# Attention stage on one Trainium2 core: the keys' mean taken from ScalarE's accumulator, eight heads' maxima placed together, and values weighed in halves in the steps without a piece

## The chip, the cores and the metric

The program runs on one core of a Trainium2 chip. The time is the device time of one execution in microseconds (us). Before the change three runs gave 1661.81, 1661.89 and 1663.59 us, so the median is 1661.89 us. One further execution was profiled; it took 1659.83 us, of which the span from the first to the last instruction is 1658.1 us. Lines of the code are named as the profile names them: L367 is line 367 of the kernel before.

## What is computed

A block of four parts runs on an input of 8 batches x 512 tokens x 256 channels: an attention that only treats the more telling queries, a routed feed-forward layer, a gated linear attention with its own feed-forward layer, and the routed layer again. The change lies in the attention alone:

```python
q, k, v = (_split_heads(x @ W + b) ...)            # 16 heads of 16 channels
scores = jnp.einsum('bhqd,bhkd->bhqk', q, k) * scale
sparsity = scores.max(axis=-1) - scores.mean(axis=-1)
_, top_idx = jax.lax.top_k(sparsity, U)            # U = 307 of 512 queries
attn = jax.nn.softmax(scores_sel, axis=-1)
out_sel = jnp.einsum('bhuk,bhkd->bhud', attn, v)   # the other queries give zero
```

The kernel does not form the mean of the scores. It takes the mean over the tokens off the keys, so that the maximum of the scores against these keys is at once "maximum minus mean".

## The kernel before

**Layout.** The 16 heads of a batch stand in two key tiles `ks[0]` and `ks[1]` and two query tiles `qs[0]`, `qs[1]` (parity e), each of two halves m of 128 rows. A half holds four blocks of 32 rows, and a block holds one head's 16 rows of that parity and one spare row. The spare row of the keys is one, the spare row of the queries takes the negated maximum, so that the score product of the second pass comes out less its maximum.

**Two passes in lockstep.** The loop at L539 runs over steps n. Step n takes the maxima (`max_one`, L415) of four heads for 128 queries: four score products on TensorE into PSUM banks of the pool `bank_m` (four banks), four maxima on VectorE (L425). The same step takes the exponentials (`exp_one`, L429) of the heads and keys of step n - 16 (`LAG`): four score products on TensorE (L433) into the pool `bank` (three banks), four exponentials on ScalarE (L437). A step sends its products in two halves of four (exp 0, max 1, exp 2, max 3; then max 0, exp 1, max 2, exp 3). The products of a half sit on the four row groups of TensorE and run side by side. Between the halves TensorE weighs the values with the exponentials of the step before (`finish`, `weigh`, L442). A batch is 16 steps; with 8 batches there are 128 steps, and then 16 more with exponentials alone.

**Pieces.** Behind each step one piece of the projections of a later batch is sent (`front`, L271): the generator yields after each piece. For a batch these are two transposes of the normalized input (`xnT`), then for m = 0 the two halves of the query projection, the mean of the keys (`km`), the two halves of the key projection, for m = 1 the same without the mean, and four pieces for the values: 15 pieces in 16 steps. I number the places behind the steps of a batch 0 to 15 (n - 14 modulo 16): before, place 4 is the mean, place 15 is empty. A projection piece is held in a bank of `bank_m` until its copy is written.

**The keys' mean before.** The copy of the transposed input on ScalarE (L298) also sums the tokens; four small products on TensorE (L344) carry the sum through the key weights; four small VectorE operations (L350 to L355) make the bias `kb`; ScalarE writes the two key tiles with it (L367).

**Placing the maxima.** When the four steps of one (m, e) are done, `place_maxima` (L396) runs two steps later: TensorE turns the 16 columns of maxima, ScalarE negates them (L403), SP issues four transfers into the spare query rows and four into `neg`, the table for the choice of the queries. It runs in the steps of places 3, 7, 11 and 15.

**Start and end.** The first 14 steps (`LEAD`) have maxima only, while the pieces of batches 0 and 1 are sent faster. In the last steps, 113 to 128, the batches to project are used up, and in three of four steps `finish` runs in two halves of 256 queries, one behind each half of the scores (`halves`, L543). After the last maximum VectorE finds the queries to drop in 26 rounds (`top_queries`, L464), while TensorE and ScalarE do the last 16 steps of exponentials; the rest of the program follows.

**Order.** Each engine runs its instructions in the order in which this code sends them. There is no reordering; what the code puts behind a waiting instruction of an engine waits too.

Of the kernel before, what the change touches and what calls it, by code (L numbers as in the profile page):

```python
# [17 lines left out]
P = 128  # L18
# [20 lines left out]
def block_kernel(ctx: ExitStack, tc: tile.TileContext, t: dict, out: bass.AP):  # L39
# [59 lines left out]
    with ExitStack() as outer:  # L99
# [20 lines left out]
        neg = a_out.tile([P, L], F32, name="neg")  # L120
        mx = a_out.tile([P, NB, NG, 4 * 4], F32, name="mx")
        work = a_out.tile([P, L + 8], F32, name="work")
        m8 = a_out.tile([P, 8], F32, name="m8")

        with ExitStack() as inner:
# [60 lines left out]
            for e in range(2):  # L186
                nc.vector.tensor_scalar(bq_own[:, e, :], bq, own[:, e : e + 1], None, ALU.mult)


# [81 lines left out]
            def front(b, pick, alone):  # L271
# [18 lines left out]
                xnT = a2.tile([P, NC2, L], F32, tag="xnT", name=f"xnT{b}")  # L290
                xsum = a2.tile([P, NC2], F32, tag="xsum", name=f"xsum{b}")
                for c in range(NC2):
                    ps = pick(f"xnT_ps{b}")
                    for k in range(4):
                        nc.tensor.transpose(
                            ps[:, bass.ts(k, P)], xn[:, k, bass.ts(c, P)], ident
                        )
                    nc.scalar.activation(  # L298
                        xnT[:, c, :], ps, AF.Identity, accum_out=xsum[:, c : c + 1]
                    )  # L300
                    yield
# [10 lines left out]
                fronts[b] = (qs, ks, va)  # L312
                kb = a2.tile([P, 2, NC2], F32, tag="kb", name=f"kb{b}")

# [6 lines left out]
                for m in range(NC2):  # L321
                    ps = pick(f"q_ps{b}")
                    for c in range(NC2):
                        project(ps, wq, m, c)
                        if c == 0:
                            yield
                    for e in range(2):
                        if alone and (b > 0 or e == 0):
                            nc.scalar.activation(
                                qs[e][:, m, :], ps, AF.Identity,  # L330
                                bias=bq_own[:, e, m : m + 1], scale=own[:, e : e + 1],
                            )
                        else:
                            nc.vector.tensor_scalar(
                                qs[e][:, m, :], ps, bq[:, m : m + 1], own[:, e : e + 1],
                                ALU.add, ALU.mult,
                            )
                    yield
                    if m == 0:

                        pm = pick(f"km_ps{b}")
                        for mm in range(NC2):
                            for c in range(NC2):
                                nc.tensor.matmul(  # L344
                                    pm[:, mm : mm + 1], wk[:, c, bass.ts(mm, P)],
                                    xsum[:, c : c + 1],
                                    start=(c == 0), stop=(c == NC2 - 1),
                                )
                        km = a2.tile([P, NC2], F32, tag="km", name=f"km{b}")
                        nc.vector.scalar_tensor_tensor(  # L350
                            km, pm[:, 0:NC2], 1.0 / L, bk, ALU.mult, ALU.add
                        )
                        nc.vector.tensor_tensor(km, bk, km, ALU.subtract)
                        for e in range(2):
                            nc.vector.tensor_scalar(  # L355
                                kb[:, e, :], km, kept[:, e : e + 1], one[:, e : e + 1],
                                ALU.mult, ALU.add,
                            )
                        yield

                    ps = pick(f"k_ps{b}")
                    for c in range(NC2):
                        project(ps, wk, m, c)
                        if c == 0:
                            yield
                    for e in range(2):
                        nc.scalar.activation(  # L367
                            ks[e][:, m, :], ps, AF.Identity,
                            bias=kb[:, e, m : m + 1], scale=kept[:, e : e + 1],
                        )  # L370
                    yield
# [23 lines left out]

            def place_maxima(b, m, e):  # L396


                q = fronts[b][0][e]
                pt = bank_m(f"mxT_ps{b}")  # L400
                nc.tensor.transpose(pt[0:16, 0:P], mx[:, b, 2 * e + m, :], ident)
                negT = a2.tile([16, P], F32, tag="negT", name=f"negT{b}")
                nc.scalar.mul(negT, pt[0:16, 0:P], -1.0)  # L403
                r = b * H + 8 * e + 4 * m
                for k in range(4):
                    nc.sync.dma_start(
                        out=q[DH * (1 - e) :: 32, m, bass.ts(k, P)],
                        in_=negT[4 * k : 4 * k + 4, :],
                    )
                for k in range(4):  # L410
                    nc.sync.dma_start(
                        out=neg[r : r + 4, bass.ts(k, P)], in_=negT[4 * k : 4 * k + 4, :]
                    )

            def max_one(b, m, e, k, j, pick):  # L415
# [9 lines left out]
                nc.vector.tensor_reduce(  # L425
                    mx[:, b, 2 * e + m, r : r + 1], s, AX.X, ALU.max
                )
# [69 lines left out]
            def maximum_of(n):  # L497

                b, m, e, k = steps[n]
                return mx[0:1, b, 2 * e + m, 4 * k : 4 * k + 1]  # L500

# [37 lines left out]
            for n in range(len(steps) + LAG + 1):  # L539
                ahead = steps[n] if n < len(steps) else None  # L540
                here = steps[n - LAG] if 0 <= n - LAG < len(steps) else None
                es = [None] * 4
                halves = 96 <= n - LAG - 1 < 112 and (n - LAG - 1) % 4 > 0  # L543
                if ahead is None:
# [30 lines left out]
                if n < LEAD:  # L575
# [6 lines left out]
                    for _ in near.get(n, ()):  # L582
                        pass
                    while done < 23 * (n + 1) // LEAD:
                        next(pieces, None)
                        done += 1
                else:
                    if n >= LAG:
                        next(later, None)
                    b, i = divmod(n - LEAD, 16)  # L590
                    if i == 0:
                        for _ in pieces:
                            pass
                        pieces = front(b + 2, bank_m, False) if b + 2 < NB else iter(())
                    next(pieces, None)

# [676 lines left out]
```

## Time and profile before

| what | value |
|---|---|
| median of three runs | 1661.89 us |
| profiled execution, its span | 1659.83 us, 1658.1 us |
| first maximum starts | 20.71 us |
| steps 0 to 13 (maxima only) | 20.7 to 65.4 us, VectorE busy 42.3 of 44.7 us |
| one batch of 16 steps | 67.4 us |
| last maxima (step 127) | from 536.6 us |
| choice of the queries on VectorE | 546 to 588 us |
| share of the span: TensorE, VectorE, ScalarE, GpSimd | 97%, 58%, 41%, 20% |

PE is TensorE's matrix products and PEld its weight loads, DVE is VectorE, ACT ScalarE, POOL GpSimd, SP the engine that issues most transfers. A line of the timeline gives start, length, engine, source line, operation, and the tile written and the tiles read. A product of 32-bit numbers appears as two instructions (x2 for one projection, x8 for four products of values). Lengths of neighbouring rows overlap, since engines start an instruction before the last one has ended; the distance from start to start is what one costs.

### The profile page before, as it was taken

Reading aid. Unit: us, or ns where it says so; the run is one execution under the profiler, and the core shown is the slowest. Engines: PE = TensorE matmul, PEld = TensorE weight load, DVE = VectorE, ACT = ScalarE, POOL = GpSimd, SP = SyncE. Lnnn points to the kernel's source line nnn. Section 1 sums busy time; section 2 is a strip of 40 time slices with the busy share of each in tenths; the row PEclk is TensorE's granted clock in tenths of the full one; section 3 lists DMA queues with packets and bytes.
Section 4 is the critical chain, followed back from the end, with each engine's and each line's share of the span. In section 5 each row is a group of like instructions: output and inputs, shape, how many; then the busy total and the mean of one; then the engine's idle time right before and its main releaser. Section 6 shows DMA issues by size and latency. Waiting matters only on the chain.

```text
span 1658.1 us, 19533 instructions
## 1 busy us (share of the span) xinstructions
PE 1605.9 (97%) x7298; PEld 823.9 (50%) x7298; DVE 968.2 (58%) x2007; ACT 680.1 (41%) x1216; POOL 334.8 (20%) x384
## 2 busy tenths in 40 slices
PE   7999999999999969999989999999999999999999
PEld 3423323333233247655564556555655655766666
DVE  6977777676666785437663566267265533344242
ACT  2366666666656814352346123622521452121110
POOL 3011111010100112114342342144233320000000
PEclk9999999999999979999999999999999999999999
DMA  3100000000000051010000001000000010011100
GB/s 108 40 2 3 3 2 3 2 3 2 2 3 3 2 164 26 6 34 13 1 1 0 1 1 27 0 0 0 1 1 1 0 26 0 20 33 37 41 26 26
DMA packets 23234, 27.55 MB, mean 17 GB/s; under 512 B 4932, under 2 KB 19684, under 8 KB 23140
## 3 DMA queue, kind: packets, MB, share of 16 engines
q1 hardware_dynamic: 22068, 24.74, 5.1%
q10 hardware_dynamic: 1072, 1.57, 0.3%
q8 instruction: 57, 0.93, 0.2%
q14 instruction: 37, 0.30, 0.1%
HBM read 21.19 MB, written 4.33 MB: 15 GB/s over the span
## 4 chain that ended last, share of the span: by engine, by line
PE 77%; DVE 14%; ACT 3%; POOL 3%; issue 2%; DMA 1%; SPq 0%; ACTq 0%; POOLq 0%; DVEq 0%
PE y_ps L891 16%; PE h_ps L911 11%; PE s L433 8%; PE s L422 8%; PE swi_ps L938 7%; PE proj_ps L1021 7%; PE av L442 7%; DVE pr L1054 2%; DVE pr L1044 2%; PE ao_ps L780 2%; DVE mx L425 2%; PE gla_y L1146 2%; PE q_ps L316 2%; PE v_ps L376 2%; PE k_ps L316 2%
## 5 line engine op out<-in xcount | busy, mean ns | idle before, releaser
L425 DVE TENSOR_REDUCE mx<-s 128x1 f32<-128x512 f32 x512 | 329.0, 684 | 129.0 <-PE s L433 83.0
L437 ACT ACTIVATE e<-s 128x512 f32<-128x512 f32 x512 | 276.1, 599 | 179.1 <-PE s L433 103.5
L422 PE MATMUL s<-k,q 32*128 32x512 f32 x1024 | 298.9, 638 | 2.5 <-ACT k L367 1.8
L433 PE MATMUL s<-q,k 32*128 32x512 f32 x1024 | 294.3, 638 | 0.4 <-DVE mx L425 0.3
L891 PE MATMUL y_ps<-w,h 128*128 128x256 f32 x1024 | 232.2, 382 | 3.5 <-DVE h L920 3.5
L911 PE MATMUL h_ps<-xnT,w 128*128 128x512 f32 x512 | 230.3, 598 | 4.1 <-ACT h L919 4.1
L891 PEld LDWEIGHTS y_ps<-w,h 128*128 128x128 f32 x1024 | 194.1, 192 | 40.9 <-issue 11.1
L911 PEld LDWEIGHTS h_ps<-xnT,w 128*128 128x128 f32 x512 | 95.5, 191 | 114.8 <-issue 106.1
L920 DVE TENSOR_TENSOR h<-h,mk 128x512 f32<-128x512 f32 x128 | 97.8, 777 | 82.2 <-ACT h L919 58.3
L442 PE MATMUL av<-e,va 128*32 128x512 f32 (+1 forms) x1120 | 141.9, 568 | 3.8 <-ACT e L437 2.4
L919 ACT ACTIVATE h<-h_ps,b 128x512 f32<-128x512 f32 x96 | 65.5, 684 | 176.9 <-PE h_ps L911 176.8
L422 PEld LDWEIGHTS s<-k,q 32*128 32x128 f32 x1024 | 89.6, 183 | 84.9 <-DVE mx L425 56.5
L896 DVE TENSOR_TENSOR xres<-xres,y_ps 128x512 f32<-128x512 f32 x48 | 32.8, 684 | 163.6 <-PE y_ps L891 149.3
L433 PEld LDWEIGHTS s<-q,k 32*128 32x128 f32 x1024 | 88.1, 183 | 80.8 <-ACT e L437 53.8
L938 PE MATMUL swi_ps<-zT,w_gate 128*128 128x512 f32 x256 | 122.0, 596 | 4.7 <-DVE h L947 4.6
L938 PE MATMUL swi_ps<-zT,w_up 128*128 128x512 f32 x256 | 121.2, 594 | 0.0
L891 PE MATMUL y_ps<-w_down,h 128*128 128x256 f32 x512 | 116.6, 380 | 0.0
L1021 PE MATMUL proj_ps<-q_w,rT 128*128 128x512 f32 x256 | 116.5, 594 | 0.0
L891 PEld LDWEIGHTS y_ps<-w_down,h 128*128 128x128 f32 x512 | 95.8, 190 | 21.1 <-issue 9.5
L944 ACT ACTIVATE h<-swi_ps 128x512 f32<-128x512 f32 x64 | 38.2, 596 | 157.4 <-PE swi_ps L938 157.3
L1071 POOL TENSOR_TENSOR o<-o,pr 128x512 f32<-128x512 f32 (+2 forms) x56 | 81.1, 1449 | 58.9 <-DVE pr L1054 56.9
L802 POOL TENSOR_TENSOR xres<-xres,b 128x512 f32<-128x512 f32 x32 | 40.0, 1268 | 245.5 <-ACT row L742 223.1
(193 smaller groups left out, 1734.6 us busy)
## 6 DMA issues: line engine op xcount, KB each, us to landing
mk<-md SPq DMA_DIRECT2D x32, 256.0 KB
xres<-in_L_attn_a_x SPq DMA_DIRECT2D x8, 512.0 KB
out<-xres SPq DMA_DIRECT2D x16, 256.0 KB
q<-negT SPq DMA_DIRECT2D x128, 2.0 KB
neg<-negT SPq DMA_DIRECT2D x128, 2.0 KB
w<-in_f_w1T SPq DMA_DIRECT2D x1, 1024.0 KB
w<-in_f_w2T SPq DMA_DIRECT2D x1, 1024.0 KB
w_gate<-in_b_w_gateT SPq DMA_DIRECT2D x1, 1024.0 KB
```

The lines of the kernel that those rows point to most:

```text
L316: nc.tensor.matmul(ps, w[:, c, bass.ts(m, P)], xnT[:, c, :], start=(c == 0), stop=(c == NC2 - 1),)
L422: nc.tensor.matmul(s, qs[e][rows, m, bass.ts(k, P)], ks[e][rows, m, :], start=True, stop=True)
L425: nc.vector.tensor_reduce(mx[:, b, 2 * e + m, r : r + 1], s, AX.X, ALU.max)
L433: nc.tensor.matmul(s, ks[e][rows, m, bass.ts(kt, P)], qs[e][rows, m, :], start=True, stop=True)
L437: nc.scalar.activation(ex, s, AF.Exp, scale=1.0 / DH**0.5)
L442: nc.tensor.matmul(av[32 * j : 32 * j + 32, queries], va[:, 8 * kt + 4 * m + j, e, :], es[j][:, queries], start=(kt == 0), stop=(kt == 3 a ...
L891: nc.tensor.matmul(y[0][:, bass.ts(i, D)], h[f][:, bass.ts(2 * u + i, P)], w[:, f, :], start=(f == 0), stop=(f == NF - 1),)
L911: nc.tensor.matmul(ps, w1[:, c, bass.ts(f, P)], xT[g][:, c, :], start=(c == 0), stop=(c == NC2 - 1),)
L920: nc.vector.tensor_tensor(hf, hf, mk[g][:, f, :], ALU.mult)
L938: nc.tensor.matmul(ps, w[:, c, bass.ts(f, P)], zT[g][:, c, :], start=(c == 0), stop=(c == NC2 - 1),)
L1021: nc.tensor.matmul(ps, rT[b // G4][:, c, bass.ts(b % G4, P)], q_w[:, c, m], start=(c == 0), stop=(c == NC2 - 1),)
L1071: nc.gpsimd.tensor_tensor(dst, dst, src, ALU.add)
```

## The change

It does three things.

1. The mean of the keys. `xnT` is copied without a sum, and the `km` piece with its products and VectorE operations is gone. Instead ScalarE first writes a key half with its bias into `ks[0]` and sums it on the way (`accum_out`), makes from the sum two biases of one column each, and then writes the two key halves as before (over the first writing). Two constants, `bk_kept` and `kept_l`, are made once at the start.
2. `place_maxima` takes both parities of a half at once: one transpose of 32 columns, one negation, then eight transfers into the queries and eight into `neg`. Only the last batch's m = 1 goes one by one. `mx` is laid out anew for it.
3. A batch has 14 pieces now. Places 6 and 14 of a batch, and all places once the batches are used up, are empty, and a step with an empty place weighs the values in halves unless it is the first of a group of four.

```diff
-                    nc.scalar.activation(
-                        xnT[:, c, :], ps, AF.Identity, accum_out=xsum[:, c : c + 1]
-                    )
+                    nc.scalar.copy(xnT[:, c, :], ps)
...
-                    if m == 0:
-                        pm = pick(f"km_ps{b}")
...
-                        yield
                     ps = pick(f"k_ps{b}")
                     for c in range(NC2):
                         project(ps, wk, m, c)
                         if c == 0:
                             yield
+                    total = a2.tile([P, 3], F32, tag="total", name=f"total{b}")
+                    nc.scalar.activation(
+                        ks[0][:, m, :], ps, AF.Identity,
+                        bias=bk[:, m : m + 1], accum_out=total[:, 2:3],
+                    )
+                    for e in range(2):
+                        nc.scalar.activation(
+                            total[:, e : e + 1], total[:, 2:3], AF.Identity,
+                            bias=bk_kept[:, e, m : m + 1], scale=kept_l[:, e : e + 1],
+                        )
                     for e in range(2):
                         nc.scalar.activation(
                             ks[e][:, m, :], ps, AF.Identity,
-                            bias=kb[:, e, m : m + 1], scale=kept[:, e : e + 1],
+                            bias=total[:, e : e + 1], scale=kept[:, e : e + 1],
                         )
                     yield
...
-            def place_maxima(b, m, e):
+            def place_maxima(b, m, es):
...
-                nc.tensor.transpose(pt[0:16, 0:P], mx[:, b, 2 * e + m, :], ident)
-                negT = a2.tile([16, P], F32, tag="negT", name=f"negT{b}")
-                nc.scalar.mul(negT, pt[0:16, 0:P], -1.0)
+                n = 16 * len(es)
+                pt = bank_m(f"mxT_ps{b}")[0:n, 0:P]
+                nc.tensor.transpose(
+                    pt, mx[:, b, m].rearrange("p e n -> p (e n)")[:, 16 * es[0] : 16 * es[0] + n],
+                    ident,
+                )
+                negT = a2.tile([32, P], F32, tag="negT", name=f"negT{b}")
+                nc.scalar.mul(negT[0:n, :], pt, -1.0)
...
+            EMPTY = (6, 14)
...
-            for _ in range(7):
+            for _ in range(6):
                 next(first)
...
-                halves = 96 <= n - LAG - 1 < 112 and (n - LAG - 1) % 4 > 0
+                batch, i = divmod(n - LEAD, 16)
+                empty = n >= LEAD and (batch + 2 >= NB or i in EMPTY)
+                halves = empty and LAG < n <= len(steps) and (n - LAG - 1) % 4 > 0
...
                 if ahead is not None and ahead[3] == 3:
-                    full.append((n + 2, ahead[0:3]))
+                    b, m, e = ahead[0:3]
+                    if b == NB - 1 and m == 1:
+                        full.append((n + 2, (b, m, (e,))))
+                    elif e == 1:
+                        full.append((n + 2, (b, m, (0, 1))))
...
-                    while done < 23 * (n + 1) // LEAD:
+                    while done < 22 * (n + 1) // LEAD:
...
-                    next(pieces, None)
+                    if not empty:
+                        next(pieces, None)
```

More of the change, by code (lines that the diff above doesn't have):

```diff
@@ L120, in block_kernel @@
         neg = a_out.tile([P, L], F32, name="neg")
-        mx = a_out.tile([P, NB, NG, 4 * 4], F32, name="mx")
+        mx = a_out.tile([P, NB, NC2, 2, 4 * 4], F32, name="mx")
         work = a_out.tile([P, L + 8], F32, name="work")
@@ L187, in block_kernel @@
                 nc.vector.tensor_scalar(bq_own[:, e, :], bq, own[:, e : e + 1], None, ALU.mult)
+            bk_kept = a1.tile([P, 2, NC2], F32, name="bk_kept")
+            kept_l = a1.tile([P, 2], F32, name="kept_l")
+            for e in range(2):
+                nc.vector.tensor_scalar(
+                    bk_kept[:, e, :], bk, kept[:, e : e + 1], one[:, e : e + 1],
+                    ALU.mult, ALU.add,
+                )
+            nc.vector.tensor_scalar(kept_l, kept, -1.0 / L, None, ALU.mult)
             vas = [
@@ L290, in front @@
                 xnT = a2.tile([P, NC2, L], F32, tag="xnT", name=f"xnT{b}")
-                xsum = a2.tile([P, NC2], F32, tag="xsum", name=f"xsum{b}")
                 for c in range(NC2):
@@ L312, in front @@
                 fronts[b] = (qs, ks, va)
-                kb = a2.tile([P, 2, NC2], F32, tag="kb", name=f"kb{b}")
                 def project(ps, w, m, c):
@@ L338, in front @@
                     yield
-                    if m == 0:
-                        pm = pick(f"km_ps{b}")
[L342 to L358, printed above, removed]
-                        yield
                     ps = pick(f"k_ps{b}")
@@ L365, in front @@
                             yield
+                    total = a2.tile([P, 3], F32, tag="total", name=f"total{b}")
[3 more added lines that the diff above has]
+                    )
+                    for e in range(2):
+                        nc.scalar.activation(
+                            total[:, e : e + 1], total[:, 2:3], AF.Identity,
+                            bias=bk_kept[:, e, m : m + 1], scale=kept_l[:, e : e + 1],
+                        )
                     for e in range(2):
@@ L394, in front @@
                     yield
-            def place_maxima(b, m, e):
-                q = fronts[b][0][e]
-                pt = bank_m(f"mxT_ps{b}")
-                nc.tensor.transpose(pt[0:16, 0:P], mx[:, b, 2 * e + m, :], ident)
-                negT = a2.tile([16, P], F32, tag="negT", name=f"negT{b}")
-                nc.scalar.mul(negT, pt[0:16, 0:P], -1.0)
[L404 to L413, printed above, removed]
+            def place_maxima(b, m, es):
[4 more added lines that the diff above has]
+                    ident,
+                )
+                negT = a2.tile([32, P], F32, tag="negT", name=f"negT{b}")
+                nc.scalar.mul(negT[0:n, :], pt, -1.0)
+                for i, e in enumerate(es):
+                    for k in range(4):
+                        nc.sync.dma_start(
+                            out=fronts[b][0][e][DH * (1 - e) :: 32, m, bass.ts(k, P)],
+                            in_=negT[16 * i + 4 * k : 16 * i + 4 * k + 4, :],
+                        )
+                for i, e in enumerate(es):
+                    r = b * H + 8 * e + 4 * m
+                    for k in range(4):
+                        nc.sync.dma_start(
+                            out=neg[r : r + 4, bass.ts(k, P)],
+                            in_=negT[16 * i + 4 * k : 16 * i + 4 * k + 4, :],
+                        )
             def max_one(b, m, e, k, j, pick):
@@ L425, in max_one @@
                 nc.vector.tensor_reduce(
-                    mx[:, b, 2 * e + m, r : r + 1], s, AX.X, ALU.max
+                    mx[:, b, m, e, r : r + 1], s, AX.X, ALU.max
                 )
@@ L499, in maximum_of @@
                 b, m, e, k = steps[n]
-                return mx[0:1, b, 2 * e + m, 4 * k : 4 * k + 1]
+                return mx[0:1, b, m, e, 4 * k : 4 * k + 1]
             def later_stats():
@@ L589, in block_kernel @@
                         next(later, None)
-                    b, i = divmod(n - LEAD, 16)
-                    if i == 0:
+                    if (n - LEAD) % 16 == 0:
                         for _ in pieces:
                             pass
-                        pieces = front(b + 2, bank_m, False) if b + 2 < NB else iter(())
-                    next(pieces, None)
+                        pieces = (
+                            front(batch + 2, bank_m, False) if batch + 2 < NB else iter(())
+                        )
+                    if not empty:
+                        next(pieces, None)
         wpool = ctx.enter_context(tc.tile_pool(name="wpool", bufs=1, side="right"))
```

## The prediction

> **What bounds the kernel now.** I read the shares by engine first (TensorE 97%), then the busy time by stretch for one batch of steps, then TensorE's own timeline there. The columns of the stretch are its length, then busy time (and instructions) of TensorE, its weight loads, VectorE, ScalarE, GpSimd, and the granted clock.
>
> ```profile
> core 0: us, PE busy (x) PEld busy (x) DVE busy (x) ACT busy (x) POOL busy (x), PEclk, DMA share, GB/s
> 267.00:334.40 67.40, 67.40 (x442) 20.89 (x444) 47.25 (x80) 41.27 (x81) 7.96 (x7) 1.00 0.01 3
> ```
>
> TensorE is never without a row, but a row also covers waiting, so this alone proves little. The Trainium skill (Perfetto Trace Analysis, "Identifying the Most-Contended Engine") says the same: matmul busy share is a bad measure, the share of weight loads (with the arithmetic done against the peak) a good one. That share is 20.89 of 67.40 us, 31%; by it TensorE has room, and taking products off it would gain nothing. So I read distances from start to start around a key piece (step 52):
>
> ```profile
> 230.83 1.12 PE L316 MATMUL k_ps<-xnT,wk 128*128 128x512 f32 x2
> 231.89 0.69 PE L433 MATMUL s<-q,k 32*128 32x512 f32 x1
> ...
> 232.96 1.07 PE L442 MATMUL av<-e,va 128*32 128x512 f32 x8
> 233.95 0.28 PE L401 MATMUL mxT_ps<-ident,mx 128*16 128x128 f32 x1
> 234.16 0.69 PE L422 MATMUL s<-k,q 32*128 32x512 f32 x1
> ```
>
> A projection piece costs 1.06 us, a half of four scores 1.07, the values 1.00, the turned maxima 0.21. These distances repeat to 0.01 us in nearly all steps. A batch, summed from them: 32 halves x 1.07 + 16 x 1.00 + 12 projection pieces x 1.06 + 2 transposes x 0.59 + the keys' mean 0.98 + 4 x 0.21 = 65.96 us. From 268.14 to 335.50 us, the same spot one batch apart, it took 67.36. So TensorE waits 1.4 us in a batch, and here the row decides against the weight-load share: work taken off TensorE is time gained. The waits sit where no piece, or only a short one, stands between two score halves. The largest is behind the empty place 15:
>
> ```profile
> 268.14 0.69 PE L422 MATMUL s<-k,q 32*128 32x512 f32 x1
> ...
> 271.05 1.06 PE L442 MATMUL av<-e,va 128*32 128x512 f32 x8
> ```
>
> Two halves take 2.91 us here instead of 2.14: a wait of 0.77, since the next half's exp products need a bank of three that ScalarE has not yet read. Behind the two transposes 0.22 and 0.24, in step 65 0.26.
>
> The end of the stage follows the last maximum at a fixed distance: the chain of waits goes from the `neg` transfer to VectorE's 26 rounds (546 to 588 us), while TensorE is done at 580.6. I therefore count only what moves the last maximum.
>
> **Part 1, what is taken off TensorE and what the halves do, per batch.** The mean: -0.98. Two of four turned maxima: -2 x 0.21 = -0.42. Place 15 now holds a value piece: its wait goes, -0.77. For the two halved steps I read step 115, where halves are used already:
>
> ```profile
> 494.34 0.64 PE L442 MATMUL av<-e,va 128*32 128x256 f32 x8
> 494.91 0.69 PE L433 MATMUL s<-q,k 32*128 32x512 f32 x1
> ...
> 496.24 0.64 PE L442 MATMUL av<-e,va 128*32 128x256 f32 x8
> ```
>
> A half of the values costs 0.57, so 1.14 for both instead of 1.00: +0.14 a step, +0.28. The following score half takes 1.33 here and 1.27 in the step before (491.43 to 492.70), instead of 1.07, because 0.57 us hides less of ScalarE's reading than a piece: about +0.23, for the step of place 14 (place 6 below). Sum: -0.98 - 0.42 - 0.77 + 0.28 + 0.23 = **-1.66 us a batch**. Steps 110 to 112 are newly halved: 3.90 us each before (474.13 to 478.03), 1.07 + 0.57 + 1.27 + 0.57 = 3.48 after, -0.42 each, with one turn less: **-1.5 us** in all.
>
> **Part 2, the new chain on ScalarE.** Behind a key piece ScalarE did this in step 52 and 53:
>
> ```profile
> 231.14 1.09 ACT L437 ACTIVATE e<-s 128x512 f32<-128x512 f32 x2 [0.58 <-PE s L433]
> 232.11 1.45 ACT L367 ACTIVATE k<-k_ps,kb,kept 128x512 f32<-128x512 f32 x2
> 233.44 1.10 ACT L437 ACTIVATE e<-s 128x512 f32<-128x512 f32 x2
> ```
>
> It goes without a gap. The first exponential of step 53 starts at 233.44, though its product was there at about 233.0, and ends near 234.06 (start to start of two is 0.48, so one lasts 0.62). The program's order of waits says who needs it: the last exp product in the second half of the same step takes the bank that this exponential reads. That half began at 234.16. The cover is 0.06 us: whatever is added to ScalarE between 232.11 and 233.44 stops TensorE at once, with every product behind it in its queue.
>
> What is added is X. The rows for it:
>
> ```profile
> L367 ACT ACTIVATE k<-k_ps,kb,kept 128x512 f32<-128x512 f32 x32 | 23.2, 782 | 5.3 <-PE k_ps L316 4.9 <-DVE kb L355 0.4
> L754 ACT ACTIVATE rT<-chT_ps,scale 128x512 f32<-128x512 f32 x16 | 10.1, 682 | 1.1 <-PE chT_ps L752 1.1
> L298 ACT ACTIVATION_READ_ACCUMULATOR xnT<-xnT_ps 128x1 f32 x16 | 3.3, 206 | 0.0
> L64 ACT ACTIVATE ln_rs<-ln_mv,eps 128x8 f32<-128x8 f32 x12 | 3.6, 299 | 34.5 <-DVE ln_mv L63 34.3
> ```
>
> The first writing has one column operand, as L754: 682 ns, about 0.57 start to start (L367 with two: 782 and 0.66). The accumulator read takes 0.21, so the sum is there at 0.78. The small biases wait for it: no row shows ScalarE waiting for itself, the nearest is VectorE's chain L350 to L355, where the next starts 0.04 after the last has ended. L64 with one column costs 0.30; with two, 0.39. The first ends at 0.82 + 0.39 = 1.21; the second overlaps it (0.2 to 0.3 later); the key writing waits for the first, 0.04: **X = 1.25 to 1.4, taken 1.35**. Bounds: not below 1.1 (0.78 and one small operation at 0.30); not above 1.8 (both small ones in full, 0.1 for each wait). No gain is possible here: nothing leaves ScalarE between those two points. The page "ScalarE: Activation LUTs" ("What ACT_TABLE_LOAD costs") gives 186 ns + 0.833 ns an element + 93 ns a column operand, 93 ns of it overlapped; with the accumulator's row that makes 0.82 + 0.28 + 0.28 and two waits of 0.04, an estimate of 1.46, or 2 x 0.11 x 6 = 1.3 us more in the final sum. I stay with the rows, as they have the start-to-start distances. The same page's rules for kernel authors speak against the change outright: adding and multiplying belong on VectorE. In these rows the small operation is no dearer on ScalarE (299 against 286 ns for L355); what the rule does not see is that ScalarE's queue holds the next exponentials.
>
> Place 10, step of place 11 (turned maxima between, values whole): stop = X - 0.07 = 1.28. Place 5, step of place 6: here the values are halved and nothing is turned, so the second half would begin at 232.96 + 0.57 = 233.53 instead of 234.16, and the stop is X + 0.56 = 1.91. (The 0.23 behind a halved step does not come on top; ScalarE has caught up.) Sum **+3.19 us a batch**. The piece's bank is freed earlier than this exponential ends, so it adds nothing.
>
> **Small parts.** At the start the chain delays the first key writing: it would begin at 18.25 (ScalarE is free of L329) + 1.35 = 19.6 instead of 18.72, +0.9; steps 0 to 13 are bound by VectorE (42.3 of 44.7 us), which loses the four `km` operations of batch 1, -0.85. Together 0, between -1 and +2. The new constants run while VectorE waits for a transfer (4.6 us idle before 15.1). The lost accumulator reads of L298 lie in ScalarE's slack. Maxima of parity 0 are placed four steps later, still seven steps (about 29 us) before use; SP issues four in 2.33 us, so eight land well inside; `neg` follows behind them, and the next placing is 34 us off. If that cover failed, exponentials would wait in the step of place 2 or 10. The end is unchanged, since the last half is placed singly.
>
> **Sum.** Six batches are projected inside the steps (2 to 7): 6 x (3.19 - 1.66) - 1.5 + 0 = **+7.7 us**. The profiled execution had 1659.83 us (span 1658.1 and 1.7 around it), so 1667.5; the median of runs is 2.1 above the profiled one, so 1669.6. Two tenths of a per cent, 3.3 us, is what can be told from no change.
>
> **Rivals.**
> - *ScalarE's slack takes the chain.* It is busy 41.27 of 67.40 us, so it has 26 us to spare, and 3 us more would vanish. Then only part 1 is left: 6 x -1.66 - 1.5 = -11.5, 1650.4 us. It decides if less than 0.71 us of X reaches TensorE (6 x (2X + 0.49 - 1.66) = 1.5). Against it: the slack lies behind the spot, not in it, and the first writing with its accumulator read is 0.74 start to start alone. Chance 0.13.
> - *A break-even*, where X reaches TensorE by 0.5 to 1.0, as the small operations overlap more than any row shows: 1658.6 to 1665.2. Chance 0.08.
> - *The chain is dearer*, each step of it exposing the whole latency of ScalarE to itself: X about 2.4 gives 6 x (5.29 - 1.66) - 1.5 = +20, 1682 us. For it: no row shows this kind of wait. Chance 0.11.
> - The forecast, X from 1.1 to 1.8: +4.6 to +13, 1666.5 to 1675. Chance 0.68.
>
> The range, 1660 to 1678, holds the forecast, the break-even and the near part of the dearer chain. Faster 0.14, same 0.07, slower 0.79.
>
> **What would show it.** In the profile after: one batch of 68.9 us instead of 67.4; no product L344; the score half behind places 5 and 10 stretched by 1.9 and 1.3 us, ended by an exponential; about 1.35 us from the start of the first writing of the keys to the first of the two that stay; place 15 without its 0.77. The forecast is wrong if the step behind place 5 takes under 4 us, or if the first maxima or the end of the stage move by more than 2 us on their own.

## The result, and the profile after

| | before | after |
|---|---|---|
| median (runs) | 1661.85 us (6) | 1670.14 us (6) |
| lowest and highest | 1660.41, 1663.59 us | 1668.79, 1672.46 us |
| profiled execution, its span | 1659.83, 1658.1 us | 1669.87, 1668.2 us |
| one batch of 16 steps | 67.4 us | 68.9 us |
| first maximum | 20.71 us | 21.62 us |
| step 126 (maxima) starts | 532.46 us | 540.12 us |

The changed kernel is slower: ratio 1.0051, 95% interval 1.0038 to 1.0064. The forecast was 1669.6 us. A step starts, here and below, with the earlier of its first maximum on VectorE and its first exponential on ScalarE.

First the stretch of one batch, in the same columns as before (length, then busy time and instructions of TensorE, weight loads, VectorE, ScalarE, GpSimd; clock):

```profile
core 0: us, PE busy (x) PEld busy (x) DVE busy (x) ACT busy (x) POOL busy (x), PEclk, DMA share, GB/s
275.55:344.45 68.90, 68.52 (x446) 21.15 (x450) 46.65 (x76) 43.38 (x84) 7.95 (x7) 1.00 0.01 3
```

TensorE has lost work, yet the batch is 1.5 us longer, and 0.38 us of it is without any TensorE row. Where that is, ScalarE's timeline shows, behind the key piece of place 5 (start, length, line, operation):

```profile
298.68 1.08 ACT L438 ACTIVATE e<-s 128x512 f32<-128x512 f32 x2 [1.08 <-PE s L434]
299.65 0.69 ACT L352 ACTIVATE k<-k_ps,bk 128x512 f32<-128x512 f32 x1
300.24 0.19 ACT L352 ACTIVATION_READ_ACCUMULATOR k<-k_ps,bk 128x1 f32 x1
300.47 0.66 ACT L357 ACTIVATE total<-total,bk_kept,kept_l 128x1 f32<-128x1 f32 x2
301.04 1.43 ACT L362 ACTIVATE k<-k_ps,total,kept 128x512 f32<-128x512 f32 x2
302.36 1.55 ACT L438 ACTIVATE e<-s 128x512 f32<-128x512 f32 x3
```

From the first writing (299.65) to the first kept writing (301.04) it takes 1.39 us here, 1.37 at the start of the program. ScalarE works without a pause, and the first exponential of step 68, which stands right behind the two kept writings, is that much later. TensorE, in the same step:

```profile
301.19 0.69 PE L423 MATMUL s<-k,q 32*128 32x512 f32 x1
301.19 0.69 PE L434 MATMUL s<-q,k 32*128 32x512 f32 x1
...
303.00 1.12 PE L434 MATMUL s<-q,k 32*128 32x512 f32 x2 [0.38 <-ACT e L438]
304.05 0.42 PE L443 MATMUL av<-e,va 128*32 128x256 f32 x4
```

(The second row of the fence is the other pass's product on its own row group; the four of a half start together when nothing stops them.) The half of four scores takes 304.05 - 301.19 = 2.86 us instead of 1.07, a stop of 1.79. The product that comes last starts at 303.00, when the exponential of 302.36 has left its bank. The same half in the step of place 11:

```profile
323.67 0.69 PE L423 MATMUL s<-k,q 32*128 32x512 f32 x1
...
324.47 0.69 PE L423 MATMUL s<-k,q 32*128 32x512 f32 x1
324.95 0.69 PE L434 MATMUL s<-q,k 32*128 32x512 f32 x1
...
326.00 0.48 PE L371 MATMUL v_ps<-wv,xnT 128*128 128x256 f32 x1
```

2.33 us instead of 1.07: a stop of 1.26. Here two products wait one after the other. The third (324.47) waits for the bank of the key piece, which the second kept writing leaves at 324.42; the fourth (324.95) waits for the exponential behind it. The weight loads of these two products show what each waited for (from 322 to 327 us: total wait, times, longest):

```profile
PEld s L423 <- ACT k L362: 0.5, 1, 0.5
PEld s L434 <- ACT e L438: 0.2, 1, 0.2
```

What the change gives is there as well. The empty place 14, then place 15, which now has a piece behind it:

```profile
337.10 0.69 PE L423 MATMUL s<-k,q 32*128 32x512 f32 x1
...
338.46 0.64 PE L443 MATMUL av<-e,va 128*32 128x256 f32 x8
339.03 0.69 PE L434 MATMUL s<-q,k 32*128 32x512 f32 x1
...
340.10 1.06 PE L443 MATMUL av<-e,va 128*32 128x512 f32 x8
341.10 0.69 PE L423 MATMUL s<-k,q 32*128 32x512 f32 x1
...
342.23 1.13 PE L371 MATMUL v_ps<-wv,xnT 128*128 128x256 f32 x4
```

In the halved step the half of scores takes 1.36 us, and the last half of the next step 1.13, so 0.29 and 0.06 of waiting are left where place 15 had 0.77.

### The profile page after: what moved, and what is told of

It is laid out like the page before. It is cut to its first block, busy times and chain, and to the rows that moved or that the text cites. A ratio compares the mean times of both kernels' runs of the same rounds, so it can differ in the third digit from the quotient of the medians.

```text
span 1668.2 us, 19554 instructions
## 1 busy us (share of the span) xinstructions
PE 1611.7 (97%) x7339; PEld 824.7 (49%) x7339; DVE 962.9 (58%) x1978; ACT 696.6 (42%) x1249; POOL 334.8 (20%) x384
## 4 chain that ended last, share of the span: by engine, by line
PE 78%; DVE 11%; ACT 5%; POOL 3%; DMA 2%; issue 1%; SPq 0%; ACTq 0%; POOLq 0%; DVEq 0%
PE y_ps L901 16%; PE h_ps L921 11%; PE s L434 9%; PE s L423 8%; PE av L443 7%; PE swi_ps L948 7%; PE proj_ps L1031 7%; DVE pr L1064 2%; DVE pr L1054 2%; PE ao_ps L790 2%; PE q_ps L321 2%; PE gla_y L1156 2%; PE v_ps L371 2%; POOL o L1081 1%; PE chT_ps L762 1%
## 5 line engine op out<-in xcount | busy, mean ns | idle before, releaser
L434 PE MATMUL s<-q,k 32*128 32x512 f32 x1024 | 303.1, 639 | 2.6 <-ACT e L438 2.3
```

The source lines that it names most:

```text
L434: nc.tensor.matmul(s, ks[e][rows, m, bass.ts(kt, P)], qs[e][rows, m, :], start=True, stop=True)
```

## The experiments

The theory: ScalarE's longer chain behind a key piece stops TensorE at two spots of each batch, 3.05 us together, and the rest of the change is a gain. The rivals: the halves cost, or the paired maxima, or the clock. "Batch" is the distance from step 94 to step 110; "last maxima" is the start of step 126 against the kernel before's 532.46 us, both in the profiled execution. Ratios are to the kernel before, run on the same chip. e1 leaves out part of the computation; the other variants do all of it.

| run | median us (before beside it) | ratio, 95% interval | batch us | last maxima us |
|---|---|---|---|---|
| before | | | 67.36 | 0 |
| after | 1670.14 (1661.85) | 1.0051 (1.0038 to 1.0064) | 68.87 | +7.66 |
| e1_no_sum | 1654.82 (1661.14) | 0.9956 (0.9941 to 0.9972) | 66.26 | -9.57 |
| e2_mean_as_before | 1655.26 (1661.14) | 0.9961 (0.9949 to 0.9973) | 66.78 | -5.04 |
| e3_chain_longer | 1685.39 (1661.14) | 1.0143 (1.0130 to 1.0156) | 71.57 | +23.35 |
| e4_singles | 1671.53 (1661.14) | 1.0065 (1.0052 to 1.0077) | 69.52 | +14.62 |
| e12_one_more | 1679.02 (1662.18) | 1.0104 (1.0090 to 1.0117) | 71.07 | +19.17 |
| e6_whole | 1681.58 (1662.18) | 1.0121 (1.0107 to 1.0135) | 71.49 | +22.47 |
| e13_bias_on_vector | 1662.53 (1662.18) | 1.0003 (0.9994 to 1.0011) | 67.60 | +1.83 |
| e8_vector_sum | 1656.60 (1662.18) | 0.9970 (0.9962 to 0.9979) | 66.06 | -1.54 |
| e15_one_between | 1668.52 (1662.36) | 1.0037 (1.0024 to 1.0049) | 68.28 | +6.22 |
| e14_best | 1659.22 (1662.36) | 0.9981 (0.9974 to 0.9988) | 66.07 | -2.41 |

**The chain taken away.**

```diff
-                    total = a2.tile([P, 3], F32, tag="total", name=f"total{b}")
-                    nc.scalar.activation(ks[0][:, m, :], ps, AF.Identity, ..., accum_out=total[:, 2:3])
-                    for e in range(2):
-                        nc.scalar.activation(total[:, e : e + 1], total[:, 2:3], ...)
...
-                            bias=total[:, e : e + 1], scale=kept[:, e : e + 1],
+                            bias=bk_kept[:, e, m : m + 1], scale=kept[:, e : e + 1],
```

> The changed kernel without the first writing of the keys, its sum and the two small biases: the two kept writings take the constant bias, so the keys' mean is not subtracted (that part of the computation is left out). Theory (ScalarE's chain stops TensorE at two spots of a batch): with X = 0 the stop in the step of place 11 is gone and that of place 6 is 0.56, so a batch is 67.4 - 1.66 + 0.56 = 66.3 us instead of 68.9, and the time about 6 x -1.10 - 2.1 (steps 110 to 112, as measured) = 8.7 us under the kernel before, near 1653. The second half of scores of the step of place 6 takes about 1.6 us instead of 2.86, that of place 11 about 1.07 instead of 2.33. Rival (the loss comes from the halved values, the paired maxima or the clock windows, not from the chain): the time stays at 1665 or above and the batch over 68 us.

The batch is 66.26 us and the step of place 11 is back at 4.37 us (4.36 before, 5.63 after). The rival is out: with halves and paired maxima kept, the loss is gone with the chain. The step of place 6 in this variant, ScalarE first, then TensorE:

```profile
224.34 1.45 ACT L352 ACTIVATE k<-k_ps,bk_kept,kept 128x512 f32<-128x512 f32 x2
225.68 1.08 ACT L428 ACTIVATE e<-s 128x512 f32<-128x512 f32 x2
```

```profile
225.87 0.69 PE L413 MATMUL s<-k,q 32*128 32x512 f32 x1
...
226.33 0.69 PE L424 MATMUL s<-q,k 32*128 32x512 f32 x1
...
227.38 0.64 PE L433 MATMUL av<-e,va 128*32 128x256 f32 x8
```

The half takes 1.51 us, a stop of 0.44 where 0.56 was forecast. With the chain it is 1.79: the difference, 1.35, is the chain's own length (1.39) but for 0.04. At place 11, where the stop without the chain is nothing, 0.13 of the chain's 1.39 us is covered. So nearly all of ScalarE's added time reaches TensorE. Behind the last maximum some of the gain is lost (-9.57 there, -6.3 in the medians), of which more below.

**The mean as before, the rest of the change kept.**

```diff
+                    if m == 0:
+                        pm = pick(f"km_ps{b}")
+                        ... (the km products and kb, as before the change)
-            EMPTY = (6, 14)
+            EMPTY = (14,)
```

> The changed kernel with the keys' mean taken as before (from the sums of the turned inputs, by four small products on TensorE), so fifteen pieces in a batch, only place 14 empty and halved; paired maxima and halves are kept. Theory: the loss is all in the chain on ScalarE, so what is left is gain: per batch -0.42 (two turns) -0.77 (place 15 filled) +0.14 (one halved step) +0.23 (wait behind it) and about +0.2 for small waits = -0.6, so 6 x -0.6 - 2.1 = about 5.9 us under the kernel before, near 1656. Batch 66.8 us. Rival (halves or pairing cost): at or above the kernel before, 1662 or more.

1655.26 us, batch 66.78: as expected. Parts 2 and 3 of the change are worth 5.9 us alone; part 1 turns them into a loss.

**The chain made longer, by two small operations and by one.**

```diff
+                    for e in range(2):
+                        nc.scalar.activation(
+                            total[:, 3 + e : 4 + e], total[:, 2:3], AF.Identity,
+                            bias=bk_kept[:, e, m : m + 1], scale=kept_l[:, e : e + 1],
+                        )
```

> The changed kernel with the two small biases computed twice (two further ScalarE operations of 128x1 into spare columns, behind the first two). Theory: everything put there reaches TensorE, so X grows by two start-to-start distances of 0.29, 0.58 us, at 12 places: +7.0, with the start's +0.6 about +7.5 us over the changed kernel, near 1677.7; a batch is 70.06 us instead of 68.9. Rival (ScalarE's slack absorbs it, and the chain is not what costs): within 1.5 us of the changed kernel, 1668.6 to 1671.6, batch 68.9.

Twice as much as the theory said: +15 us over the changed kernel. In the one batch whose steps keep full clock (steps 30 to 46) it lost 1.12 us, where 1.16 was expected: from 72.08 to 73.20. In the others there is more, behind the stop of place 6. TensorE there, then the clock (the column before the last two) in a short stretch:

```profile
311.43 1.12 PE L439 MATMUL s<-q,k 32*128 32x512 f32 x2 [0.94 <-ACT e L443]
312.48 0.64 PE L448 MATMUL av<-e,va 128*32 128x256 f32 x8
313.05 0.86 PE L439 MATMUL s<-q,k 32*128 32x512 f32 x1
...
314.73 1.94 PE L448 MATMUL av<-e,va 128*32 128x512 f32 x8
316.60 0.80 PE L428 MATMUL s<-k,q 32*128 32x512 f32 x1
```

```profile
core 0: us, PE busy (x) PEld busy (x) DVE busy (x) ACT busy (x) POOL busy (x), PEclk, DMA share, GB/s
314.60:315.00 0.40, 0.40 (x8) 0.20 (x8) 0.16 (x1) 0.20 (x1) 0.08 (x1) 0.50 0.02 5
```

The values take 1.87 us from start to start instead of 1.00: the clock is granted at half. Steps of places 6 and 7 together take 11.36 us instead of the 9.77 of the batch with full clock, so one such window of 3.41 us costs 1.6 us, and there were five in six batches. In the profiled execution the six batches are 14 us longer than those of the changed kernel, 8 by the windows and 6 by the chain, and the start is 2.1 us later. The windows are a cost which no rival had. To see where it begins, one operation less:

```diff
-                    for e in range(2):
+                    for e in range(1):
                         nc.scalar.activation(
                             total[:, 3 + e : 4 + e], ...
```

> The changed kernel with one of the two small biases computed a second time (the run with two extra lost 15 us instead of 7.5: its trace has a half-clock window of 3.41 us behind five of six steps of place 6, where the stop had grown from 1.8 to 2.4 us, and none behind place 11, where it had grown from 1.26 to 1.8). Theory (the stop lengthens by what is put into the chain, and a stop of TensorE somewhere between 1.8 and 2.4 us makes the clock fall to half): stop of 2.1 us at place 6, 1.55 at place 11, so +3.5 +0.3 = 3.8 us over the changed kernel, near 1674, if 2.1 us is still short enough, or up to +8 more, near 1682, with half-clock windows behind place 6, if it is not. Rival (the dear part of the longer chain was each small operation itself, 0.6 us apiece, clock apart): steps of place 11 grow by over 0.5 us and the time is +7.5 without such windows.

+8.9 us. The step of place 11 grew by 0.28 us (5.63 to 5.91), the step of place 6 by 0.27 where the clock stayed, so each operation costs its start-to-start distance and no more. Half-clock windows stand behind place 6 in three of six batches. The stop there is 1.79 us in the changed kernel (0.38 of it without a row; no window in six batches), 2.07 here (0.66 without a row; three of six), 2.35 in the run before (0.94; five of six). The changed kernel is thus one small operation away from a second loss as large as the first. The Trainium skill (TensorE: Matmul & The Clock Gate, Part 1) has windows of 3.4 us that run freely, which fits: in each profile all changes of the clock lie on one grid of 3.41 us, and the batches differ in where the stop falls on it. Its table of states lets the clock fall after a whole idle window, while a later section of the same part has frequent short idle times between groups of products bring it down too, without a figure. Here the windows came behind stops of 2.1 us with 0.66 us without a row, far from a whole idle window; the measurement decides. But the time without a row is not the measure either: near 197 us the changed kernel's TensorE has 1.60 us without a row, in a wait for ScalarE, and near 195 us the kernel before has 1.18, and the clock stays full behind both. What is counted stays open.

**The maxima placed singly.**

```diff
-                    if b == NB - 1 and m == 1:
-                        full.append((n + 2, (b, m, (e,))))
-                    elif e == 1:
-                        full.append((n + 2, (b, m, (0, 1))))
+                    full.append((n + 2, (b, m, (e,))))
```

> The changed kernel with the maxima turned and placed one parity at a time again (four turns a batch instead of two). Theory (pairing saves two turns of 0.21 us on TensorE in a batch, and nothing else): 6 to 7.5 x 0.42 = +2.5 to +3.2 us over the changed kernel, near 1673; batch 69.3 us. Rival A (the turn lies inside ScalarE's stop where it falls behind a key piece, so it is free there): only one of the two turns costs, +1.3. Rival B (the later placing in pairs delays queries, or SP's eight transfers together are in the way): no difference, or faster than the changed kernel.

The batch is 0.65 us longer (69.52): 0.21 in the step of place 7, 0.43 in that of place 15, where the turn moves the next half of scores and its wait grows from 0.06 to 0.25. So each turn saved counts, the second one double. The medians are only 1.4 apart, and the profiled execution of this run was its slowest, late by 3.8 us more than the changed kernel's at step 14 already; its start has 13.65 us at half clock, that of the changed kernel 3.41. The sum of a whole run is here too coarse to tell 1.3 from 3; the batches tell it.

**The values whole at places 6 and 14.**

```diff
-                halves = empty and LAG < n <= len(steps) and (n - LAG - 1) % 4 > 0
+                halves = batch + 2 >= NB and LAG < n <= len(steps) and (n - LAG - 1) % 4 > 0
```

> The changed kernel with the values weighed whole in the steps of places 6 and 14 (halves only once the batches are used up). Theory: behind the key piece the halves move the second half of scores 0.43 us forward into the same stop, and only cost the extra 0.14 and a later start: the step of place 6 becomes about 4.65 us instead of 5.07; at place 14 the halves fill a wait: places 14, 15 and 0 together become about 11.83 us instead of 11.53. Net -0.1 to -0.2 us a batch: within 1.5 us of the changed kernel. Rival (halves are what costs): -0.6 us a batch or more, 4 us or more faster than the changed kernel.

Neither: 11.4 us slower than the changed kernel. My expectation took it that ScalarE has caught up after the first stop. It has not:

```profile
239.09 0.69 PE L423 MATMUL s<-k,q 32*128 32x512 f32 x1
...
240.47 1.18 PE L434 MATMUL s<-q,k 32*128 32x512 f32 x2 [0.25 <-ACT e L438]
...
242.61 0.69 PE L434 MATMUL s<-q,k 32*128 32x512 f32 x1 [0.53 <-ACT e L438]
...
243.67 0.64 PE L443 MATMUL av<-e,va 128*32 128x512 f32 x4
```

Behind an empty place two halves of scores follow each other, with no half of the values between, and take 4.58 us instead of 2.14, a stop of 2.44, of which 0.25 and 0.53 us are without a row. Without a half-clock window places 6 and 7 lose 0.51 us a batch, places 14 to 0 lose 0.49 (12.02 instead of 11.53), and in four of six batches a half-clock window comes on top. The halves are what keeps the changed kernel's stop short enough.

**The small biases on VectorE.**

```diff
                     for e in range(2):
-                        nc.scalar.activation(total[:, e : e + 1], total[:, 2:3], AF.Identity, ...)
+                        nc.vector.tensor_scalar(
+                            total[:, e : e + 1], total[:, 2:3],
+                            kept_l[:, e : e + 1], bk_kept[:, e, m : m + 1], ALU.mult, ALU.add,
+                        )
```

> The changed kernel with the two small biases computed by VectorE instead of ScalarE (the sum stays with ScalarE's first writing). Theory (what counts is the time between the exponentials and the first kept writing, whichever engine computes): the sum stands at about 0.85 us, a wait from engine to engine each way of some 0.05 to 0.1 and one VectorE operation of about 0.3 make X 1.2 to 1.4, and VectorE's queue holds the next maxima behind the wait; time within 2 us of the changed kernel, 1668 to 1672. Rival (small operations are at home on VectorE, so the loss goes with them): X under 0.9 and 5 us or more faster than the changed kernel.

The rival was right about the time: 7.6 us faster than the changed kernel, no change against before. ScalarE's and VectorE's timelines at place 6 show why:

```profile
230.43 0.69 ACT L352 ACTIVATE k<-k_ps,bk 128x512 f32<-128x512 f32 x1
231.02 0.19 ACT L352 ACTIVATION_READ_ACCUMULATOR k<-k_ps,bk 128x1 f32 x1
231.48 0.60 ACT L439 ACTIVATE e<-s 128x512 f32<-128x512 f32 x1 [0.27 <-PE s L424]
231.98 1.44 ACT L363 ACTIVATE k<-k_ps,total,kept 128x512 f32<-128x512 f32 x2
```

```profile
231.25 0.45 DVE L357 TENSOR_SCALAR total<-total,kept_l,bk_kept 128x1 f32<-128x1 f32 x2 [0.60 <-ACT k L352]
```

The built program has one exponential ahead of the two kept writings, although the code sends it behind them; I had said of the order that nothing is moved, and that does not hold: in this variant ScalarE's order differs from the code's behind every key piece inside the steps, in the changed kernel behind one (step 24). So two things changed, the engine and the order. To part them, the biases went back to ScalarE and one exponential was sent between by hand:

```diff
+                    def write_keys(m=m, ps=ps, total=total): ...  # the two kept writings
+                    if alone: write_keys()
+                    else: owed.append(write_keys)
...
                                 es[i] = exp_one(*here, i, bank)
+                                while owed:
+                                    owed.pop(0)()
```

> The changed kernel with one exponential placed on ScalarE between the two small biases and the two kept writings, in the batches projected inside the steps; the biases stay on ScalarE. This is the order in which ScalarE ran in the variant with the biases on VectorE, which was 7.6 us faster than the changed kernel. Question: does that gain come from the order or from the engine? Theory (order: what stops TensorE is the first exponential behind the whole lump; split by one exponential the lump costs at most half): the first exponential ends 0.3 to 0.4 us later than with the biases on VectorE, so steps of places 6 and 7 together take 8.4 to 8.9 us instead of 9.22, place 11 5.3 to 5.6 instead of 5.63; 3 to 7 us faster than the changed kernel, 1663 to 1667. Rival (the engine: what helped is ScalarE rid of 0.6 us of small operations): within 1.5 us of the changed kernel, 1668.6 to 1671.6.

Between the two, nearer to the rival: 1.6 us faster in the medians. In the profiled executions the six batches gain 3.4 us, and a start that is 1.9 us later takes most of it back. Steps of places 6 and 7 together take 8.63 us instead of 9.22, inside the expected span, but the step of place 11 stays at 5.64:

```profile
323.41 0.69 PE L430 MATMUL s<-k,q 32*128 32x512 f32 x1
...
324.69 0.69 PE L430 MATMUL s<-k,q 32*128 32x512 f32 x1 [0.15 <-ACT k L364]
...
325.75 0.48 PE L378 MATMUL v_ps<-wv,xnT 128*128 128x256 f32 x1
```

There the wait for the exponential has gone and the wait for the key piece's bank has taken its place: the third product starts 1.28 us after the first, where it was 0.80 in the changed kernel, since the kept writings now start later; 1.28 is just when the fourth started there. The turned maxima take a bank too, which may be why a product of this half gets the piece's and none does at place 6; this was not tried. Of the 1.27 us that a batch with the biases on VectorE is shorter, the order gives 0.59 and the engine, which brings the kept writings forward, 0.68.

**The whole mean on VectorE, and the kept writings later.**

```diff
+                        nc.vector.tensor_reduce(total[:, 2:3], ps, AX.X, ALU.add)
+                        for e in range(2):
+                            nc.vector.tensor_scalar(total[:, e : e + 1], total[:, 2:3],
+                                kept_l[:, e : e + 1], one[:, e : e + 1], ALU.mult, ALU.add)
...
-            EMPTY = (6, 14)
+            EMPTY = (2, 8)
...
+                        while half == 0 and owed:   # between the first exponentials and the values
+                            owed.pop(0)()
```

> The changed kernel with the keys' mean of batches 2 to 7 taken by VectorE (one sum over the finished product and two small operations, no first writing), the two kept writings issued between the halves of the next step, behind its first two exponentials, and the empty places 2 and 8 instead of 6 and 14, so that no turned maxima follow a key piece. Theory: ScalarE's queue never waits for a mean; both stops go, TensorE still has one piece and two turns less. Batch 65.9 to 66.4 us, so 6 x (-1.0 to -1.5) - 2.1 + 0.9 is 7 to 10 us under the kernel before, 1651 to 1654. Rival (the product's bank is held longer, and the fourth bank taken after it waits for ScalarE's writings; or VectorE's maxima come late): stops of 0.5 us or more in both steps, batch over 67 us, no faster than the variant with the mean as before (1655).

These lines hold for batches 2 to 7; batches 0 and 1 keep the chain on ScalarE.

```profile
275.09:341.17 66.08, 66.08 (x446) 20.21 (x450) 48.35 (x82) 40.79 (x77) 7.98 (x7) 1.00 0.01 3
116.00:118.00 2.00, 2.00 (x4) 0.50 (x2) 0.69 (x1) 0.60 (x1) 0.00 (x0) 0.50 0.01 3
```

The batch (first row, columns as above) is what was expected, 66.06 us, the shortest of all. But the first batch inside the steps lost 3.4 us (steps 14 to 30), most of it in the step of place 11, 8.05 us under half clock (second row), and the start 2.1; so the median, 1656.60, misses its expected 1651 to 1654. An attempt to mend both:

```diff
-                empty = n >= LEAD and (batch + 2 >= NB or i in EMPTY)
+                empty = n >= LEAD and (batch + 2 >= NB or i in (EMPTY if batch else FIRST))
+            FIRST = (10, 14)
...
+                    if alone:   # batches 0 and 1: xsum, km and kb as before the change
```

> The variant with the sum on VectorE, with two changes: batches 0 and 1, which are projected ahead of the exponentials, take the mean as the kernel before (products on TensorE), so that the start is as before; and the first batch inside the steps has its empty places at 10 and 14 instead of 2 and 8, since in that variant the step of place 11 there fell together with the waits of the late statistics and a half-clock window (8.05 us instead of 4.54). Theory: start +0.1, the first batch within 0.5 us of the kernel before, then five batches of 66.06 instead of 67.37 (-6.5), steps 110 to 112 -2.1: 8 to 9 us under the kernel before, 1652 to 1654. Rival (the lost time at the start and in the first batch lies in the VectorE work itself, or half-clock windows turn up elsewhere): no better than 1656.

The rival: 1659.22. The first batch loses 3.5 us again, with a half-clock window in the same steps, and the start is 1.2 us late although its mean is computed as before. Step 24, the one before, is longer than the other steps of its place in every variant, in the kernel before by 2.7 us (6.97 instead of 4.24). ScalarE is busy there with late statistics: from 107.62 to 110.53 us it loads the table for their square root, takes the root, and loads the table for the exponentials again (1.28, 0.30 and 1.28 us), and the exponentials wait. That something added next to this stop brings the clock down is likely, but was not tried by itself. The lowest median with the whole computation stays that of the mean on TensorE, 1655.26 us, ahead of both the kernel before and the change; the sum on VectorE, with 1656.60, cannot be told from it, as the intervals of the two ratios overlap.

## Why the prediction was right

The mechanism held: the chain stops TensorE at the two places forecast, by a wait for the exponential behind it, and the rest of the change is a gain. That the sum came within 0.6 us of the measured median is in part luck. In the profiled execution the six batches cost 8.9 us instead of 9.2 and the start 0.9 instead of 0, and the steps from 110 on gave back 2.1 instead of 1.5; these errors cancel to +7.66 against +7.7.

- **TensorE bounds the stage, and time off it is gained.** Held: e2 has less work and less waiting on TensorE and nothing new on ScalarE, and its batch is 0.58 us shorter; in e1, which has the km products off as well, it is 1.10 shorter. The weight-load share, one of the two measures that the Trainium skill (Perfetto Trace Analysis, "Identifying the Most-Contended Engine") goes by, was 31% and would have said that there is nothing to gain.
- **X, from 1.25 to 1.4, taken 1.35.** Measured 1.37 at the start, 1.39 at place 5 (the rows of steps start a little later), and 1.35 as the difference of two stops (1.79 with the chain, 0.44 without). The estimate by the Trainium skill (ScalarE: Activation LUTs, "What ACT_TABLE_LOAD costs") had been 1.46. The unknown wait of ScalarE for itself was 0.03 us. The same page's rule that adding and multiplying belong on VectorE, which I had weighed as beside the point, pointed the right way: the two small operations took 0.45 us there instead of 0.66, and the engine was worth 0.68 us a batch.
- **The cover of 0.06 us.** The stop of place 11 was forecast at X - 0.07 = 1.28 and measured 1.26. But with X measured 1.39 there the cover was 0.13: the prediction's own rows gave 0.10 (from 234.06 to 234.16), not 0.06, and the error in X made up for it. That the piece's bank "adds nothing" held only because the exponential is later by 0.5 us; e15 shows it waiting right behind.
- **Place 6, forecast 1.91.** Mis-sized by 0.12: the part which comes from the halves was 0.44, not 0.56. The wait behind the halved place 14 was mis-sized the other way, 0.35 instead of 0.23. The two cancel, and the batch is 68.9 us as forecast.
- **Steps 110 to 112, forecast -1.5.** -1.6 by step 113 (each takes 3.43 to 3.48 us, as forecast), but step 113 behind them is shorter too, 3.51 us instead of 4.13, which was not in the sum: from step 110 to step 126 the shift went from +9.79 to +7.66, -2.1.
- **Start, forecast 0.** +0.94 at step 14. The +0.9 at the first key writing came as forecast; the 0.85 that VectorE saves did not come back. In e1, which saves it too and has no chain, step 14 is 1.10 us early, 0.35 of it at the first maximum, so the saving is real; what the changed kernel's profile has besides is a half-clock window of 3.41 us at about 22 us, which was not in the sum. Over all profiles step 14 moves with the half-clock time ahead of it: -1.1 to +0.1 us without any (e1, e2), +0.9 to +2.9 with 3.41 us (the changed kernel and four variants), +2.4 and +3.0 with 6.83, +4.7 and +4.9 with 10.24 or more. That the clock takes this time is likely; what brings it down there was not tried.
- **The last maxima:** +7.66 against +7.7. **The end, forecast unchanged:** the profiled execution grew by 10.04 us, 2.4 more than at step 126. Over all variants the part behind step 126 is -0.6 to +4.0 us against the profile of the kernel before, whose own profiled execution was 2.0 us below its median. TensorE's half-clock stretches behind the attention differ, 10.24 and 6.83 us in the kernel before, 10.24 and 13.65 after, but do not account for it: e14 has as much as the changed kernel, 23.89 us, and its part behind step 126 grew by 0.2 us. The cause stays open. The medians, 8.3 us apart, lie nearer to the sum.
- **The rivals.** Slack that takes the chain is refuted by e1 and e3: at most 0.13 us of what is put into this spot is absorbed. The dearer chain (1682) has the time that e3 and e6 reached, but by a mechanism I had not thought of: a clock that falls behind the stop.

## What to carry to other kernels

Idle time of an engine says nothing about one spot in its queue: ask which instruction stands behind the new work, which bank it frees, and who waits for that bank. If that cover is a tenth of a microsecond, nearly the whole added latency is paid, even on an engine that is a third idle. And before reordering to remove such a wait, look for the second wait right behind it, here the piece's own bank, for it takes the place of the first.

## What was not expected of the hardware

- Behind a stop of TensorE of 2.1 us (0.66 us without any row) the clock fell to half for a window of 3.41 us in three of six batches, behind one of 2.35 us (0.94) in five, behind one of 1.8 us (0.38) in none. One window cost 1.6 us. Yet 1.60 us without any row at another spot was followed by none.
- Copying the 128 x 512 table `neg` on VectorE, ahead of the choice of the queries, took 1.15 us before and 0.45 us after (1.00 in e3, 0.45 to 0.47 in the other variants); it gave 0.7 us back behind the last maxima. Why is open.
